# A two-layer graph network on one core: the routed experts' surroundings worked by groups of tiles, layer 1 fed from DRAM, edge terms as pairs of 64 rows in two places

## The chip, the cores and the metric

The kernel runs on one core of a Trainium2 chip. The core has five engines with a queue each, worked in order: PE (matrix products and transposes), DVE (vector work from SBUF and PSUM), ACT (copies, activations, and DMA issues), POOL (here mostly indirect DMAs: row gathers and scatters) and SP (DMA issues). [...] The metric is the device time of one execution in microseconds (us), the median of the runs. All data and arithmetic here is f32. The engines' instruction streams are written in program order by the kernel's Python and scheduled at build: an instruction waits for a semaphore of what it depends on, and whatever stands behind it on its engine waits too.

## The reference

3125 nodes with 256 features, 100,000 edges sorted by destination, 64 attributes an edge. Two layers, each a residual block of graph network plus mixer, then a residual feed-forward block:

```
xn = layernorm(x)
x  = x + L0_gnn(xn, edges) + L0_mix(xn)            # layer 0
x  = x + L0_ffn(layernorm(x))                      # 16 experts, top 2
xn = layernorm(x)
x  = x + L1_gnn(xn, edges, edge_attr) + L1_mix(xn) # layer 1
x  = x + L1_ffn(layernorm(x))                      # half of the tokens
```

The expert block, for each token y (normed x):

```
logits = y @ gate_w + gate_b ; the two largest, softmax over the two -> w
moe    = sum over the two experts of w * (relu(y @ w1[e] + b1[e]) @ w2[e] + b2[e])
out    = layernorm(y + moe) * gamma + beta
```

Layer 1's graph network, 8 heads of 32:

```
q = xn@Wq.T + bq ; k = xn@Wk.T + bk ; v = xn@Wv.T + bv ; e = edge_attr@We.T
alpha = sum(q[dst] * (k[src] + e)) / sqrt(32), softmax over the edges of one dst -> w
out   = sum over edges of w * (v[src] + e)  +  xn@Wskip.T + bskip
```

Layer 1's mixer is a second-order attention: moments of keys and of pairs of keys with the values are summed over all nodes (eight heads, worked as two halves of 128 columns), then each node's query reads them; a projection is added to x.

## The kernel before

**Tiling.** The nodes form 25 tiles of 125, in seven groups (`k.groups`) of up to four tiles. The residual x lies in SBUF for the whole kernel as `xcur` [125, 25, 256].

**Layer 0** (0 to some 3607 us) is not touched except that what follows it queues on SP and POOL behind its last loads, stores and row gathers, where the loads of the next stage are issued among them.

**The expert block**, `l0_ffn_routed` (line 1442), works in stages that each finish all tiles before the next begins:
1. Statistics and norm of all 25 tiles into `acc`, transposes to `xT` (`ln_to_T`, line 108).
2. Gate: per tile three small products and a copy (`gate_logits`, line 1425), PE and DVE in turn.
3. Top 2 of 16 for all tiles (`top2`, line 1393); a product with a triangular matrix and one with ones give each token its position in its expert's list; `sloti` holds its row in `xs`, a DRAM table of 16 × 512 rows.
4. 50 scatters (line 284): tile by tile and choice by choice, POOL sends the 125 rows of `acc` to `xs`.
5. 16 experts: loads of the two weight matrices, of `b2` and of the expert's 512 rows `xe` (line 1523 transposes them), two products with a relu between, result stored to `ys` in DRAM. The row loads wait for all scatters.
6. 50 gathers from `ys` (line 1552), each into one of three buffers of 125x256, followed by a DVE multiply-add into `acc`.
7. `norm_into` (line 1559): statistics of all tiles, then per tile norm (DVE, line 103), gamma (DVE, 1572), beta (POOL, 1573) and the add into `xcur` (POOL, 1574).

**Between the blocks** `layer1` (line 2496) norms again, stores the rows to DRAM (`xtab`) and keeps the transposed columns `xT` in SBUF. `l1_gnn_slots` (line 1889) first makes the k/v table: per tile a product, a DVE add of the bias (line 1923), and per group a store of up to 1000 KB to `kvtab`, from two buffers.

**The slot stage** (4244 to 6641 us, `by_slots`, line 876). The nodes are sorted by degree into 25 tiles of 128 with a fixed number of edge slots each (`SLOTS`, 64 down to 22); in all 864 slots, worked in 64 steps of up to 16 slots. Per step and block of up to 8 slots:
- POOL gathers a k/v row per node and slot (line 637) into one of four buffers `kv` [128, 8, 512]; the step's edge attributes come by one gather `ea`.
- For each pair of slots `add_edges` adds e = edge_attr @ We.T to both k and v: a PE transpose of 128x128 (two slots × 64 attributes, line 1945), an ACT copy to SBUF (1947), a PE product of 128x512 (1948) with `weT`, and a DVE add over 128x1024 (1953). `weT` is [128, 2, 256]: We in rows 0 to 63 for the first slot, in rows 64 to 127 for the second, zeros elsewhere. The product's tile `e` [128, 2, 256] is one bank by its size; the pool `e_pe` has two buffers of it, and the transpose is written to the same tile's first 128 columns.
- DVE multiplies by q (928), sums per head (932), and after softmax pieces (max, ACT exp, sum at 955) multiplies v (961) and folds it in half (966); PE sums the slots in `acc` with identity products (968).

A tile's rows for q and skip are gathered from `xtab` and transposed in the same pool's buffer (line 861 copies them).

**Beside** the slots runs the mixer, `l1_mix_pairs` (line 2201), a generator whose units are issued between the steps: it reads `xT` (SBUF) for k, v and q, keeps its moments in PSUM (`pairs`, `mom`), and adds its result to `xcur` (line 2414). Its products of 32-row blocks stand at line 2388; line 1968 is the graph network's skip product.

**Finish.** `finish` loads the graph network's result from DRAM (`gout`), seven `part` loads of 500 KB, and adds it to `xcur`; then the last feed-forward block (6681 to 6989 us).

[...]

Of the kernel before, what the change touches and what calls it, by code (L numbers as in the profile page):

```python
# [107 lines left out]
def ln_to_T(k, pool, pp, src, dstT, g=None, b=None, keep=None, rows=None):  # L108
# [4 lines left out]
    for g0, ng in k.groups:  # L113
# [7 lines left out]
        if rows is not None:  # L121
            nc.sync.dma_start(tok(rows)[:, g0 : g0 + ng], xh[:, :ng])
# [1270 lines left out]
def top2(k, one, lg):  # L1393


    nc, NT, NE = k.nc, k.NT, 16
    io = one.tile([P, NE], F32, name="io")
    nc.gpsimd.iota(
        io, pattern=[[1, NE]], base=-64, channel_multiplier=0, allow_small_or_imprecise_dtypes=True
    )  # L1400
    iob = io.unsqueeze(1).to_broadcast([P, NT, NE])
    oh = [one.tile([P, NT, NE], F32, name=f"oh{r}") for r in range(2)]
    mx = [one.tile([P, NT], F32, name=f"mx{r}") for r in range(2)]
    at = one.tile([P, NT], F32, name="at")
    for r in range(2):
        nc.vector.tensor_reduce(mx[r], lg, axis=AX.X, op=ALU.max)
        nc.vector.tensor_tensor(
            oh[r], lg, mx[r].unsqueeze(2).to_broadcast([P, NT, NE]), op=ALU.is_equal
        )
        nc.vector.tensor_tensor(oh[r], oh[r], iob, op=ALU.mult)  # L1410
        nc.vector.tensor_reduce(at, oh[r], axis=AX.X, op=ALU.min)
        nc.vector.tensor_tensor(
            oh[r], iob, at.unsqueeze(2).to_broadcast([P, NT, NE]), op=ALU.is_equal
        )
        if r == 0:
            nc.vector.scalar_tensor_tensor(lg, oh[0], -BIG, lg, op0=ALU.mult, op1=ALU.add)
# [5 lines left out]
    return oh, mx  # L1422
# [19 lines left out]
def l0_ffn_routed(k, dram, xcur, a, over):  # L1442
# [3 lines left out]
    NE = 16  # L1446
    ns = CAP // 128
    xs = dram.tile([NE * CAP, D], F32, name="xs")
    ys = dram.tile([NE * CAP, D], F32, name="ys")
    with ExitStack() as st:  # L1450
        big, one, wts, wp, hp, pp = pools(
            k, st, [("f_big", 1), ("f_one", 1), ("f_w", 3), ("f_wk", 3), ("f_hid", 2)], [("f_ps", 2)]
# [7 lines left out]
        xT = big.tile([128, 2, N], F32, name="xT")  # L1460
        ln_to_T(k, wp, pp, xcur, xT, keep=acc)
        lg = gate_logits(k, pp, one, xT, a)
        oh, mx = top2(k, one, lg)

# [6 lines left out]
        sel = one.tile([P, NT, NE], F32, name="sel")  # L1471
        nc.vector.tensor_tensor(sel, oh[0], oh[1], op=ALU.add)
        flat = sel.rearrange("p i e -> p (i e)")
        within = pp.tile([128, 512], F32, name="tp", tag="tp")
        nc.tensor.matmul(within[:P, : NT * NE], tri, flat, start=True, stop=True)
        total = pp.tile([128, 512], F32, name="o", tag="o")
        nc.tensor.matmul(total[:P, : NT * NE], ones, flat, start=True, stop=True)
# [5 lines left out]
        for i in range(NT):  # L1483
            nc.vector.tensor_tensor(
                base[:, i + 1], total[:P, i * NE : i * NE + NE], base[:, i], op=ALU.add
            )
        full = one.tile([P, NE], F32, name="full")
# [3 lines left out]
        pos = one.tile([P, NT, NE], F32, name="pos")  # L1491
        nc.vector.tensor_tensor(
            pos.rearrange("p i e -> p (i e)"), within[:P, : NT * NE],
            base[:, :NT].rearrange("p i e -> p (i e)"), op=ALU.add,
        )
        slot = one.tile([P, 2, NT], F32, name="slot")
        sloti = one.tile([P, 2, NT], I32, name="sloti")
        for r in range(2):
            nc.vector.tensor_tensor(oh[r], oh[r], pos, op=ALU.mult)
            nc.vector.tensor_reduce(slot[:, r], oh[r], axis=AX.X, op=ALU.add)  # L1500
        nc.vector.tensor_scalar_min(slot, slot, NE * CAP - 1.0)
        nc.vector.tensor_copy(sloti, slot)
        index = [sloti[:, r, i : i + 1] for i in range(NT) for r in range(2)]
        sent = scatter_rows(k, xs, index, [acc[:, i] for i in range(NT) for r in range(2)])
# [3 lines left out]
        stored = []  # L1508
        for e in range(NE):
# [26 lines left out]
            for i in range(ns):  # L1536
                ps = pp.tile([128, 512], F32, name="o", tag="o")
                for j in range(4):
# [5 lines left out]
            stored.append(  # L1544
                nc.scalar.dma_start(
                    ys[e * CAP : e * CAP + CAP, :].rearrange("(p i) d -> p i d", p=128), ye
                )
            )
        for i in range(NT):
            for r in range(2):  # L1550
                g = wp.tile([P, D], F32, name="g", tag="g")
                nc.gpsimd.indirect_dma_start(
                    out=g, out_offset=None, in_=ys,
                    in_offset=bass.IndirectOffsetOnAxis(ap=sloti[:, r, i : i + 1], axis=0),
                )
                nc.vector.scalar_tensor_tensor(
                    acc[:, i], g, mx[r][:, i : i + 1], acc[:, i], op0=ALU.mult, op1=ALU.add
                )
        norm_into(k, one, wp, acc, xcur, a)
# [20 lines left out]
def l0_ffn(k, xcur, a):  # L1580
    nc, N, NT = k.nc, k.N, k.NT
    NE = 16
    with ExitStack() as st:
# [11 lines left out]
        oh, mx = top2(k, one, lg)  # L1595
# [293 lines left out]
def l1_gnn_slots(k, dram, xT, xtab, xcur, order, edge_attr, a, beside):  # L1889

    nc, N = k.nc, k.N
    kvtab = dram.tile([N, 2 * D], F32, name="kvtab3")
    gout = dram.tile([len(SLOTS) * 128, D], F32, name="gout3")
    sent = []
    with ExitStack() as st:
        (one,) = pools(k, st, [("e_one", 1)])

# [4 lines left out]
        weT = one.tile([128, 2, D], F32, name="weT")  # L1902
        nc.gpsimd.memset(weT, 0.0)
        for b in range(2):
            nc.sync.dma_start(weT[b * 64 : b * 64 + 64, b], a["We"])
        with ExitStack() as s2:
            pw, wp, pp = pools(k, s2, [("e_pw", 1), ("e_st", 2)], [("e_pps", 4)])
            wkv = pw.tile([128, 2, 2 * D], F32, name="wkv")
            bkv = pw.tile([P, 2 * D], F32, name="bkv")
            for j, nm in enumerate("kv"):  # L1910
                nc.sync.dma_start(
                    wkv[:, :, j * D : j * D + D], a["W" + nm].rearrange("(c p) m -> p c m", p=128)
                )
                nc.sync.dma_start(bkv[:, j * D : j * D + D], a["b" + nm].partition_broadcast(P))
            for g0, ng in k.groups:
                t = wp.tile([P, 4, 2 * D], F32, name="st", tag="st")
                for j in range(ng):
                    i = g0 + j
                    ps = pp.tile([128, 512], F32, name="mm", tag="mm")
                    row_matmul(  # L1920
                        k, ps[:P], lambda c: xT[:, c, i * P : i * P + P], lambda c: wkv[:, c], None, 2
                    )
                    nc.vector.tensor_tensor(t[:, j], ps[:P], bkv, op=ALU.add)
                nc.sync.dma_start(tok(kvtab)[:, g0 : g0 + ng], t[:, :ng])

        with ExitStack() as s2:
            ep, kp, gp, wp, pe, po, pq = pools(
                k, s2,
                [("e_ea", 2), ("e_k", 2), ("e_g", 4), ("e_wk", 2)],
                [("e_pe", 2), ("e_po", 1), ("e_qa", 1)],  # L1930
            )

# [262 lines left out]
def l1_mix_pools(k, st):  # L2195
    return pools(
        k, st, [("q_one", 1), ("q_wk", 2), ("q_x", 1), ("q_sq", 3)], [("q_ps", 1), ("q_a", 1), ("q_b", 1)]
    )


def l1_mix_pairs(k, xT, xcur, a, pl):

# [415 lines left out]
```

## Time and profile before

| what | us |
|---|---|
| median of three runs (lowest, highest) | 6989.09 (6963.92, 7031.13) |
| profiled execution | 6991.24 |
| its span | 6989.4 |
| layer 0 | 0 to 3607 |
| norm, gate, top 2, positions | 3607 to 3691 |
| scatters, load of the first rows | 3691 to 3772 |
| 16 experts | 3772 to 4024 |
| gathers | 4024 to 4110 |
| norm, norm and transposes, k/v table | 4110 to 4244 |
| slot stage with the mixer | 4244 to 6641 |
| finish | 6641 to 6681 |
| last feed-forward block | 6681 to 6989 |

Over the span PE is busy 69%, DVE 63%, POOL 43%, ACT 22%; the mean granted PE clock is 0.80 of full speed. How to read the views that follow: in a row of windows each engine has its busy time and its number of instructions in that stretch; "PEclk" is the granted clock. A row of a tile or group gives line, engine, operation, output and inputs by the program's names, count; then busy time and mean ns of one, then the engine's idle time just before these instructions and who ended it. A wait reads: engine, what it wanted, who released it: sum in us, count, longest. A timeline row: start, duration, instruction; in brackets the idle time ahead of it and its releaser. An f32 product is recorded as two passes (x2, and x864 for 432 products).

### The profile page before, as it was taken

The numbers are of one execution on the slowest core, as the hardware profiler recorded it, in microseconds if no ns is written. First come the engines' busy times: TensorE is split into PE (matmuls) and PEld (weight loads), VectorE is DVE, ScalarE is ACT, GpSimd is POOL, SyncE is SP. The second block draws the span as 40 slices with busy tenths as digits, with TensorE's granted clock in tenths as the row PEclk, the third lists the DMA queues.
The fourth block names the chain that finished last, engine by engine and source line by source line (L and its number), as shares of the span: only waits on it lengthen the run. The fifth ranks groups of instructions, "written<-read, shape, count | busy, mean of one in ns | idle before, by whom it ended". The sixth has DMA issues, their size and how long they took to land. (4 is left out here: it accounts for less than half of the span.)

```text
span 6989.4 us, 48160 instructions
## 1 busy us (share of the span) xinstructions
PE 4802.1 (69%) x15661; PEld 2724.5 (39%) x15661; DVE 4388.0 (63%) x6132; ACT 1553.8 (22%) x3122; POOL 2991.1 (43%) x3084
## 2 busy tenths in 40 slices
PE   3445786577855687667834917777787787777738
PEld 2233554344533455444522602333333333333315
DVE  5367677666657777776731154656777765777771
ACT  2111223222412233323320101222112222212111
POOL 2456565555464565555433043333434433443310
PEclk9766898788877898788956957778778888888769
DMA  4356555555454565555433324333334433343310
GB/s 135 97 156 181 157 166 164 155 155 147 146 170 143 166 177 171 157 166 160 151 131 100 118 78 128 114 100 98 113 96 119 118 101 102 114 117 112 102 40 19
DMA packets 358262, 898.56 MB, mean 129 GB/s; under 512 B 93718, under 2 KB 150650, under 8 KB 357876
## 3 DMA queue, kind: packets, MB, share of 16 engines
q0 software_dynamic: 241376, 750.90, 37.1%
q1 hardware_dynamic: 109236, 123.30, 5.5%
q10 hardware_dynamic: 7390, 21.19, 0.8%
q8 instruction: 127, 2.08, 0.1%
q14 instruction: 133, 1.09, 0.1%
HBM read 816.51 MB, written 78.50 MB: 128 GB/s over the span
## 5 line engine op out<-in xcount | busy, mean ns | idle before, releaser
L637 POOL DMA_INDIRECT kv<-kvtab,slots x2592 | 2521.2, 973 | 2425.5 <-PE acc L968 827.4
L928 DVE TENSOR_TENSOR kv<-kv,qa 128x2048 f32<-128x2048 f32 (+1 forms) x351 | 741.3, 2114 | 327.4 <-DMA kv<-kvtab,slots 252.6
L1953 DVE TENSOR_TENSOR kv<-kv,e 128x1024 f32<-128x1024 f32 x432 | 519.4, 1214 | 361.4 <-PE e L1948 218.6
L932 DVE TENSOR_REDUCE al<-kv 128x32 f32<-128x2048 f32 (+3 forms) x351 | 738.2, 2112 | 1.5
L1948 PE MATMUL e<-weT,eaT 128*128 128x512 f32 x864 | 560.9, 746 | 184.7 <-ACT eaT L1947 110.4
L968 PE MATMUL cps<-kv,ident 128*128 128x256 f32 x1728 | 508.0, 449 | 155.3 <-DVE kv L966 91.4
L961 DVE TENSOR_TENSOR kv<-kv,qa 128x2048 f32<-128x2048 f32 (+1 forms) x234 | 489.5, 2113 | 0.0
L968 PEld LDWEIGHTS cps<-kv,ident 128*128 128x128 f32 x1728 | 378.5, 227 | 273.4 <-DVE kv L966 105.6
L142 PE MATMUL mm<-w,hid 128*125 128x256 f32 x1600 | 397.7, 399 | 57.9 <-issue 33.9
L1339 PE MATMUL mm<-hTm,w 128*128 128x500 f32 (+1 forms) x896 | 383.2, 586 | 25.0 <-issue 13.8
L966 DVE TENSOR_TENSOR kv<-kv 128x1024 f32<-128x1024 f32 (+1 forms) x351 | 389.2, 1134 | 0.0
L142 PEld LDWEIGHTS mm<-w,hid 128*125 128x125 f32 x1600 | 309.4, 197 | 141.7 <-issue 70.6
L1948 PEld LDWEIGHTS e<-weT,eaT 128*128 128x128 f32 x864 | 157.4, 218 | 410.4 <-issue 214.7
L968 PE MATMUL acc<-kv,ident 128*128 128x256 f32 x864 | 252.1, 454 | 70.1 <-DVE kv L966 69.6
L1339 PEld LDWEIGHTS mm<-hTm,w 128*128 128x128 f32 x896 | 173.7, 208 | 211.8 <-issue 183.8
L968 PEld LDWEIGHTS acc<-kv,ident 128*128 128x128 f32 x864 | 195.6, 232 | 154.0 <-DVE kv L966 103.6
L961 DVE TENSOR_TENSOR kv<-kv,al 128x2048 f32<-128x2048 f32 (+1 forms) x117 | 243.5, 2118 | 0.0
L142 PE MATMUL mm<-wqv,hTm 128*125 128x512 f32 x400 | 235.0, 698 | 12.2 <-DVE qs L1259 5.7
L1947 ACT COPY eaT<-e 128x128 f32<-128x128 f32 x432 | 107.2, 268 | 568.8 <-PE e L1945 269.1
L899 PE MATMUL qa<-wq,xpT 128*128 128x256 f32 x300 | 111.7, 506 | 133.5 <-ACT xpT L861 51.0
L972 ACT COPY res<-cps 128x256 f32<-128x256 f32 x128 | 47.6, 372 | 649.3 <-PE cps L968 433.3
L2388 PE MATMUL w<-x,sel 32*128 32x500 f32 (+3 forms) x448 | 161.9, 647 | 30.2 <-ACT sq L2393 14.8
(391 smaller groups left out, 7603.1 us busy)
## 6 DMA issues: line engine op xcount, KB each, us to landing
kv<-kvtab,slots POOLq DMA_INDIRECT x2592
w<-in_L_ffn_w_dram SPq DMA_DIRECT2D x32, 512.0 KB
qd<-qT ACTq DMA_DIRECT2D x24, 500.0 KB
kvtab<-st SPq DMA_DIRECT2D x12, 1000.0 KB
qT<-qd SPq DMA_DIRECT2D x24, 500.0 KB
w<-in_L_mix_W_dram SPq DMA_DIRECT2D x8, 1024.0 KB
xs<-zero SPq DMA_DIRECT2D x16, 512.0 KB
xe<-xs SPq DMA_DIRECT2D x16, 512.0 KB
```

What stands on the lines that cost most here:

```text
L142: nc.tensor.matmul(ps, lhs(c), w(c), start=(c == 0), stop=(bias is None and c == n_chunks - 1))
L637: return k.nc.gpsimd.indirect_dma_start(out=out, out_offset=None, in_=table, in_offset=bass.IndirectOffsetOnAxis(ap=index, axis=0),)
L899: nc.tensor.matmul(q, xpT[:, ci], wq[:, ci], start=(ci == 0), stop=False)
L928: nc.vector.tensor_tensor(kv[:, :m, :D], kv[:, :m, :D], q.unsqueeze(1).to_broadcast([128, m, D]), op=ALU.mult,)
L932: nc.vector.tensor_reduce(al[:, b0 : b0 + m], hv(kv[:, :m, :D]), axis=AX.X, op=ALU.add)
L961: nc.vector.tensor_tensor(v, v, w3[:, b0 : b0 + m].unsqueeze(3).to_broadcast([128, m, heads, d]), op=ALU.mult,)
L966: nc.vector.tensor_tensor(v, v, kv[:, m // 2 : m, D:], op=ALU.add)
L968: nc.tensor.matmul(acc[:, :D], k.ident, kv[:, j, D:], start=(b0 + j == 0), stop=(kv is bufs[-1][2] and j == m // 2 - 1),)
L1339: nc.tensor.matmul(ps[:, :w_], w1[:, c, j * 128 : j * 128 + 128], hT[:, c, :w_], start=(c == 0), stop=(c == 1),)
L1948: nc.tensor.matmul(e.rearrange("p b d -> p (b d)"), eaT, weT.rearrange("p b d -> p (b d)"), start=True, stop=True,)
L1953: nc.vector.tensor_tensor(t, t, e.unsqueeze(2).to_broadcast([128, 2, 2, D]), op=ALU.add)
L2388: nc.tensor.matmul(ps[:f, b, :w_], sel[rows, t * 128 : t * 128 + f], qT[rows, :w_], start=True, stop=True, tile_position=((h0 + b) * 32, 0),)
```

## The change

- **Expert block by groups.** Stages 1 to 4 above run group by group: statistics, norm, transposes, gate (the group's logits in one PSUM tile), top 2, positions (running sums `base`), and at once the group's eight scatters. Stages 6 and 7 too, with all that follows: per group eight gathers (eight buffers `f_back`), multiply-adds, statistics, norm with gamma and the add into `xcur` as two fused DVE operations, store of x, norm, store of rows, transposes, store of columns, k/v product and bias, store of k/v. Beta is added to `xcur` ahead of the experts, by seven POOL operations. The weights for k/v are loaded in front.
- **Layer 1 from DRAM.** `xcur` and `xT` are given up: the mixer loads each group's columns (`xTg`) and x (`xg4`) from DRAM and stores x back; the finish loads x beside `part` (three buffers for two).
- **Six gather buffers** `kv` in the slot stage, for four.
- **Edge terms.** `weT` holds We twice, without zeros, [128, 256]; the product of a pair is two products, rows 0 to 63 and rows 64 to 127, 256 columns each, into two banks. In place of two buffers there is one tile of two banks, `ee`, with two places of half of each bank, used in turn.

```diff
+        for g0, ng in k.groups:
+            g = slice(g0, g0 + ng)
+            mv, rs = group_stats(k, gp, xcur[:, g], ng)
+            for j in range(ng):
+                ln_tile(k, acc[:, g0 + j], xcur[:, g0 + j], mv, rs, j)
+            xT = group_T(k, gp, pp, acc[:, g], ng)
...
+            oh = top2(k, gp, io, lg, [m[:, g] for m in mx])
...
+            for i in range(g0, g0 + ng):
+                for r in range(2):
+                    ins = nc.gpsimd.indirect_dma_start(
+                        out=xs, in_=acc[:, i], in_offset=None,
+                        out_offset=bass.IndirectOffsetOnAxis(ap=sloti[:, r, i : i + 1], axis=0),
+                    )
...
+        for g0, ng in k.groups:
+            x = xcur[:, g0 : g0 + ng]
+            nc.gpsimd.tensor_tensor(x, x, bet.unsqueeze(1).to_broadcast([P, ng, D]), op=ALU.add)
...
+        for gi, (g0, ng) in enumerate(k.groups):
+            g = slice(g0, g0 + ng)
+            for i in range(g0, g0 + ng):
+                for r in range(2):
+                    got = bp.tile([P, D], F32, name="g", tag="g")
+                    gather(k, got, ys, sloti[:, r, i : i + 1])
                     nc.vector.scalar_tensor_tensor(
+                        acc[:, i], got, mx[r][:, i : i + 1], acc[:, i], op0=ALU.mult, op1=ALU.add
+                    )
+            mv, rs = group_stats(k, gp, acc[:, g], ng)
+            for j in range(ng):
+                i = g0 + j
+                nc.vector.scalar_tensor_tensor(
+                    acc[:, i], acc[:, i], mv[:, j, 0:1], gam, op0=ALU.subtract, op1=ALU.mult
+                )
+                nc.vector.scalar_tensor_tensor(
+                    xcur[:, i], acc[:, i], rs[:, j : j + 1], xcur[:, i], op0=ALU.mult, op1=ALU.add
+                )
+            nc.sync.dma_start(tok(tabs.x)[:, g], xcur[:, g])
...
+            nc.sync.dma_start(tok(tabs.rows)[:, g], acc[:, g])
+            xT = group_T(k, gp, pp, acc[:, g], ng)
+            nc.scalar.dma_start(tabs.cols[gi, :, :, : ng * P], xT[:, :, : ng * P])
...
+            nc.sync.dma_start(tok(tabs.kv)[:, g], t[:, :ng])
...
-                [("e_ea", 2), ("e_k", 2), ("e_g", 4), ("e_wk", 2)],
-                [("e_pe", 2), ("e_po", 1), ("e_qa", 1)],
-            )
+                [("e_ea", 2), ("e_k", 2), ("e_g", 6), ("e_wk", 2)],
+                [("e_pe", 1), ("e_po", 1), ("e_qa", 1)],
+            )
+            ee = pe.tile([128, 2, 2, D], F32, name="e")
+            turn = [0]
+            def place():
+                turn[0] ^= 1
+                return ee[:, :, turn[0]]
...
-                        e = pe.tile([128, 2, D], F32, name="e", tag="e")
+                        e = place()
                         nc.tensor.transpose(e[:, 0, :128], ea[:, c0 : c0 + 128], k.ident)
                         eaT = kp.tile([128, 128], F32, name="eaT", tag="eaT")
                         nc.scalar.copy(eaT, e[:, 0, :128])
-                        nc.tensor.matmul(
-                            e.rearrange("p b d -> p (b d)"), eaT, weT.rearrange("p b d -> p (b d)"),
-                            start=True, stop=True,
-                        )
+                        for b in range(2):
+                            half = slice(b * 64, b * 64 + 64)
+                            nc.tensor.matmul(e[:, b], eaT[half], weT[half], start=True, stop=True)
...
+            qT = unit_T(load_cols(gi, ng), c, ng, s, temp[:, c : c + 1])
+            x = ip.tile([P, 4, D], F32, name="xg4", tag="xg4")
+            nc.sync.dma_start(x[:, :ng], tok(tabs.x)[:, g0 : g0 + ng])
...
+                nc.vector.tensor_tensor(x[:, j], ps[:P, :D], x[:, j], op=ALU.add)
+            nc.sync.dma_start(tok(tabs.x)[:, g0 : g0 + ng], x[:, :ng])
...
+            k.nc.sync.dma_start(x[:, g0 : g0 + ng], tok(tabs.x)[:, g0 : g0 + ng])
+            after(k, k.nc.sync.dma_start(part[:, :ng], tok(gout[0 : k.N, :])[:, g0 : g0 + ng]), sent)
```

## The prediction

> **What bounds the kernel now.** I cut the span at the borders that the order of work draws and read the stages by windows first, because the page's averages mix them:
>
> ```profile
> core 0: us, PE busy (x) PEld busy (x) DVE busy (x) ACT busy (x) POOL busy (x), PEclk, DMA share, GB/s
> ...
> 3691.00:3772.00 81.00, 0.00 (x0) 0.00 (x0) 0.00 (x0) 0.00 (x0) 59.63 (x50) 0.50 0.33 90
> 3772.00:4024.00 252.00, 241.13 (x896) 160.80 (x896) 47.88 (x96) 45.25 (x65) 0.61 (x2) 0.99 0.39 128
> 4024.00:4116.00 92.00, 0.00 (x0) 0.00 (x0) 38.63 (x103) 0.32 (x1) 60.57 (x50) 0.50 0.32 79
> 4181.00:4244.00 63.00, 48.14 (x101) 19.69 (x101) 16.03 (x48) 3.94 (x11) 3.87 (x4) 0.86 0.37 133
> 4244.00:6641.00 2397.00, 1845.91 (x5396) 806.03 (x5396) 1658.34 (x1702) 507.64 (x1107) 944.65 (x976) 0.81 0.38 109
> ```
>
> To be seen: around the experts (3772 to 4024, PE full) lie two stretches in which PE does nothing and POOL's row transfers run alone, 81 and 92 us. The slot stage of layer 1 (4244 to 6641) is a third of the time, and no engine is full in it: PE 77%, DVE 69%.
>
> Then the two transfers, by tile:
>
> ```profile
> L284 POOL DMA_INDIRECT xs<-acc,sloti x50: 1184/1188/1414, 3691.1 to 3764.5; - x50
> L1552 POOL DMA_INDIRECT g<-ys,sloti x50: 1207/1211/1267, 4023.9 to 4109.5; - x50
> ```
>
> The scatters start 84 us after layer 0 ends (3607), since top-2 is done for all tiles at once; after the last gather come layer norms, transposes and the k/v table, to 4244.
>
> For the slot stage: its costly groups, DVE's and POOL's waits, and one pair in the timeline.
>
> ```profile
> L1948 PE MATMUL e<-weT,eaT 128*128 128x512 f32 x864 | 560.9, 746 | 184.7 <-ACT eaT L1947 110.4 <-issue 66.4 <-DMA kv<-kvtab,slots 6.4
> L1953 DVE TENSOR_TENSOR kv<-kv,e 128x1024 f32<-128x1024 f32 x432 | 519.4, 1214 | 361.4 <-PE e L1948 218.6 <-issue 52.9 <-remote 37.1
> ```
> ```profile
> DVE kv L1953 <- PE e L1948: 218.6, 86, 15.9
> DVE kvt L2273 <- PE pairs L2306: 63.8, 11, 18.4
> DVE den L955 <- ACT al L954: 45.0, 22, 7.7
> ...
> POOL kv L637 <- PE acc L968: 827.4, 53, 29.7
> ```
> ```profile
> 6386.88 0.27 PE L1945 MATMUL e<-ident,ea 128*128 128x128 f32 x1
> 6387.35 0.27 ACT L1947 COPY eaT<-e 128x128 f32<-128x128 f32 x1
> 6387.68 1.13 PE L1948 MATMUL e<-weT,eaT 128*128 128x512 f32 x2 [0.52 <-ACT eaT L1947]
> 6388.96 1.21 DVE L1953 TENSOR_TENSOR kv<-kv,e 128x1024 f32<-128x1024 f32 x1
> ```
>
> DVE idles 2397 − 1658 = 739 us here, half of it (361.4) before the edge adds, which wait for PE's edge product: DVE and PE take turns in a chain of transpose, copy, product, add, 432 times. POOL waits for buffers (827.4), but DVE hardly ever for a gather.
>
> **The change, part by part.** All against the profiled 6991.24 (span 6989.4 and 1.8 around it), 2.2 above the median 6989.09.
>
> *Ahead of the experts.* Per group of four tiles there are now stats, norm, transposes, gate, top-2, positions and at once eight scatters. The first group's chain: DVE about 10.4 us by the rows of these operations in 3607–3691, PE's gate 4 × 1.47 = 5.9, the rest transposes, two table loads on ACT (1.28 each) and hand-overs; I take 32 from layer 0's end at 3607, so the first scatter starts near 3639. DVE's 6.25 × 10.4 = 65 us then lie beside POOL's 50 scatters (1.19 and 0.30 until the next, 74.4). POOL also gets seven adds of beta (125x1024, 2.34 in such an add of layer 0), of which four stand ahead of the last scatters: 9.4. End 3639 + 74.4 + 9.4 = 3723; from the last scatter to PE's first transpose 6.5 as now (3765.7 to 3772.2): 3730 for 3772, **−42**. SP now has eight more loads ahead of layer 0's last stores and the experts' weights: up to 16 us late, I take 5. Together **−37**, bounds −60 (the first group takes little more than DVE's 10.4) and −10 (six more groups cost POOL 3 us each, and the loads their 16).
>
> *Behind the experts.* Now 220.6 us from 4023.9 to the first kv gather at 4244.5: gathers 86, norm 27, transposes 38, k/v table 52, 12 until its last store can be read, and hand-overs. After: DVE per tile two gathered adds 0.97, two statistics 1.17, two fused norm operations 0.98, a norm 0.41, the bias add 0.68: 4.2, × 25 = 105, and 7 + 5 + 12 to get in, drain and land: 129, −92. Against it the stores: on SP's queue x, rows and k/v, 12.8 MB where it has 9.6 now, and 3.2 of columns on ACT's; this is how the k/v store paces DVE now:
>
> ```profile
> 4208.02 2.48 DVE L1923 TENSOR_TENSOR st<-mm,bkv 125x512 f32<-125x512 f32 x4 [7.09 <-DMA kvtab<-st]
> 4216.03 2.48 DVE L1923 TENSOR_TENSOR st<-mm,bkv 125x512 f32<-125x512 f32 x4 [5.53 <-DMA kvtab<-st]
> ```
>
> 1000 KB in 8.0 us; SP's 12.8 MB make 102 us at that, and the gathers and columns share the DMA engines: 135, −85. I take **−85**, bounds −110 (gathers 86 and 24 behind them) and −50 (stores and gathers one after the other: 102 + 60.6, and the entry of 7).
>
> *Edge products.* Removed is half of each: the 128x512 product against a weight padded with zeros (two passes, 560.9 ÷ 432 = 1.30 a pair) becomes two 64-row products of 256 columns. That row blocks run side by side and 256 columns take half is seen here:
>
> ```profile
> 6399.24 1.03 PE L1968 MATMUL acc<-wsk,xpT 128*128 128x256 f32 x4
> 6407.83 2.04 PE L2388 MATMUL w<-x,sel 32*128 32x500 f32 x4 [0.69 <-ACT sq L2393]
> 6411.60 2.08 PE L1948 MATMUL e<-weT,eaT 128*128 128x512 f32 x2
> ```
>
> Each f32 product is two passes. Two products of 256 columns on 128 rows take 1.03, at a granted clock of 1.00 (window 6396 to 6400), one of 512 columns 1.13 at the same clock above. At 0.50 (6407 to 6414) two products of 500 columns on two 32-row blocks take 2.04, what one full one takes, 2.08: the blocks run beside each other. So a pair costs 0.65, **−280 us of PE's work**. This is not time yet: PE isn't full, and most of its work lies beside DVE's.
>
> Added is a wait. Before, two edge tiles of two banks each alternate: 416 of 432 transposes wait for the add of two pairs back. Now both places lie in one tile, each with half of both banks, and in the built program all 432 transposes wait for the add just before. What queues behind that transpose on PE: the mix's products, the folds into acc (which free POOL's buffers) and the next chunk's. So a loop from add to add replaces the alternation: transpose start to product end was 1.93 in the pair above, at full clock; with 0.60 for 1.13 it is 1.40, with a hand-over at each end about 1.6, at a clock of 0.50 about 2.2, with something queued ahead on PE or ACT 2.4 to 3. DVE can do other work in it: in the new DVE order only 65 of 431 adds follow another directly (111 before). Summing over all gaps what is missing with the row means of the DVE work that lies in each: idle 183 us for a loop of 1.6, 327 for 2.4, 474 for 3.0, 608 for 3.5. Against 361.4 now that is −178, −34, +113, +247. I take 2.4, the row's 1.93 shortened but queued on PE at two thirds load: −34.
>
> [...]
>
> Other DVE waits for PE and ACT (63.8 + 45.0 above and small ones, some 115) get shorter with 15% less work in PE's queue, and with adds that stand apart: I take **−40**, bounds 0 and −100.
>
> *Six gather buffers for four.* DVE's waits for kv gathers are some 12 us in the stage; nothing beyond the freedom that the new order already shows: 0, bounds −30 and 0.
>
> *Columns and x from DRAM.* The mix loads 28 column tiles and 14 x tiles of 500 KB and stores 14, 28 MB beside the stage's 2397 × 109 = 261 MB; the DMA share of 0.38 hides them. Two buffers, so a load has one unit to come; if 42 loads are late by some 0.4 us each, 5% of the 8.0 us that 1000 KB take: +15, bounds 0 and +60.
>
> Slot stage: −34 − 40 + 15 = **−60**, bounds −280 (all of PE's work returned) and +215.
>
> *Finish.* Now 40 us with seven loads of part; x has to be loaded too, 3.2 MB more on the same queue. In layer 0's tail a group with two loads takes 8.9 us: 7 × 8.9 = 62 less what the FFN's start hides, **+15**, bounds 0 and +30.
>
> Sum: 6991 − 37 − 85 − 60 + 15 = **6824**.
>
> **The rivals.**
> (a) PE is the real bound of the slot stage and returns all: −280 for −60, 6604. For: PE 77%, DVE's idle time names it. Against: the wait on the add puts DVE into PE's queue 432 times.
> (b) The other side: the two places act as one and the loop is 3.5 long because the transpose sits in PE's queue behind mix work that itself waits, so that DVE stands still in each gap. 608 − 361 = +247 in the stage, the rest −107: 7131. It decides from a loop of 3.0 (+113 cancels the rest). For: all 432 waits; the span from transpose start to product end has a median of 3.0 and a mean of 4.2 in this trace, with queueing. Against: DVE's new order puts other work into five gaps of six, and the PE queue gets shorter.
> (c) The change doesn't do what it says: the two 64-row products run one after the other, no PE work saved, four weight loads for two. Loop 2.8 to 2.9: idle 423 to 430, +65, others 0: 6991 − 107 + 65 = 6949. Against: the 32-row blocks above.
> (d) The surroundings give little: stores, columns and gathers collide, front −10, back −50, finish +30, with −30 in the slot stage: 6931.
>
> **How the numbers follow.** Forecast 0.52 (its own range 6720 to 6920), (a) 0.15, (b) 0.13, (c) 0.12, (d) 0.08. A measurement of this kernel tells 1% from no change: faster is under 6919, slower over 7059. Faster: nearly all of the forecast and (a), 0.65; same: (c), (d) and crumbs, 0.23; slower: (b), 0.12. The range runs from 6600, with (a), to 7010, with (c) and (d); (b) is left out.
>
> **What would show it.** First scatter near 3640, experts from about 3730, first kv gather about 135 us after the experts. Edge product two passes in about 0.6 us side by side. Idle before the edge add near 330; if over 470, (b). PE busy about 280 less in the slot stage; if not, (c). Waits of PE for columns above 60 us in all, or experts waiting for weights, would make it wrong too.

## The result, and the profile after

The changed kernel takes 7351.93 us (median of four runs, 7330.31 to 7373.28). The kernel before, run beside it, took 7005.14 (6963.92 to 7031.13). The ratio is 1.0501, 95% interval [1.0432, 1.0569]: **5% slower**, where 6824 was forecast. The profiled execution took 7330.31, its span 7328.4, 339 us more than the 6989.4 of before.

Where they came from, measured between the same events in both traces (layer 0's end is PE's last product before its long pause; the slot stage runs from the first edge add to the end of the last):

| stretch | before | after | change | forecast |
|---|---|---|---|---|
| layer 0's end to the experts' first product | 225.1 | 187.2 | −38 | −37 |
| experts | 246.4 | 246.5 | 0 | 0 |
| experts' end to the first edge add | 231.6 | 192.3 | −39 | −85 |
| slot stage | 2365.6 | 2807.2 | **+442** | −60 |
| finish and last feed-forward block | 373.6 | 370.3 | −3 | +15 |

The missing −22 is layer 0, which ended at 3525 for 3547. That isn't the change: five later profiles with the same surroundings, in series of the same length, had it at 3548 to 3576.

So the whole loss lies in the slot stage. Its windows after, the columns as before:

```profile
3525.00:3712.00 187.00, 55.78 (x229) 49.38 (x229) 66.70 (x285) 19.53 (x36) 91.66 (x67) 0.50 0.31 92
3712.00:3959.00 247.00, 241.34 (x896) 160.77 (x896) 48.02 (x100) 43.98 (x64) 0.00 (x0) 0.99 0.36 125
3959.00:4151.00 192.00, 80.97 (x173) 34.95 (x173) 90.83 (x298) 16.32 (x39) 73.56 (x62) 0.71 0.49 152
4151.00:6958.00 2807.00, 2142.87 (x6228) 930.11 (x6229) 1673.44 (x1683) 513.07 (x1100) 935.76 (x966) 0.67 0.35 102
```

The last row holds both surprises: PE's busy time in the stage rose (2143 us; in the same stretch of before, 4250 to 6616, it was 1829 at a clock of 0.81), though half of each edge product was taken away, and its granted clock fell to 0.67. DVE did the same work as before (1673 to 1636) in 441 us more.

The groups of the page for that stage, edge add, edge product and edge transpose:

```profile
L2043 DVE TENSOR_TENSOR kv<-kv,e 128x1024 f32<-128x1024 f32 x432 | 525.6, 1217 | 838.6 <-PE e L2041 349.0
...
L2041 PE MATMUL e<-weT,eaT 64*128 64x256 f32 x1728 | 442.6, 587 | 99.7 <-ACT eaT L2038 65.0
...
L2036 PE MATMUL e<-ident,ea 128*128 128x128 f32 x432 | 173.6, 402 | 320.3 <-DVE kv L2043 239.0
```

DVE's idle time ahead of the edge adds is 838.6 us for 361.4: that is the loss. And PE stands 239.0 us before transposes until an add is done, where before it hardly waited for one:

```profile
PE e L1945 <- DVE kv L1953: 31.1, 29, 3.4
```

The timeline after shows how the loop turns, near the stage's end (start, duration, instruction, idle time before it and its releaser):

```profile
6945.20 0.48 PE L2036 MATMUL e<-ident,ea 128*128 128x128 f32 x1 [1.40 <-DVE kv L2043]
6945.71 0.27 ACT L2038 COPY eaT<-e 128x128 f32<-128x128 f32 x1 [3.19 <-PE e L2036]
...
6946.03 1.22 PE L2041 MATMUL e<-weT,eaT 64*128 64x256 f32 x4 [0.35 <-ACT eaT L2038]
6947.36 1.22 DVE L2043 TENSOR_TENSOR kv<-kv,e 128x1024 f32<-128x1024 f32 x1
...
6948.64 0.48 PE L2036 MATMUL e<-ident,ea 128*128 128x128 f32 x1 [1.38 <-DVE kv L2043]
```

One engine works at a time: transpose, copy, products, add, then the next transpose 0.06 us after the add's end. The round takes 3.44 us, with nothing else in PE's queue, and PE runs at half clock (granted 0.50 from 6944 to 6950). A transpose behind a pause of PE takes 0.33 at full clock in this trace, 0.48 here; the four product passes 0.70 (at 5060, granted 1.00) and 1.22: 0.67 of the 3.44 us are the half clock's.

### The profile page after: what moved, and what is told of

The parts are those of the page before. It is cut to its first block, busy times and chain, and to the rows that moved or that the text cites. A ratio compares the mean times of both kernels' runs of the same rounds, so it can differ in the third digit from the quotient of the medians.

```text
span 7328.4 us, 50159 instructions
## 1 busy us (share of the span) xinstructions
PE 5115.8 (70%) x16549; PEld 2854.3 (39%) x16549; DVE 4414.9 (60%) x6270; ACT 1576.1 (22%) x3152; POOL 2977.2 (41%) x3040
## 5 line engine op out<-in xcount | busy, mean ns | idle before, releaser
L2043 DVE TENSOR_TENSOR kv<-kv,e 128x1024 f32<-128x1024 f32 x432 | 525.6, 1217 | 838.6 <-PE e L2041 349.0
L2041 PE MATMUL e<-weT,eaT 64*128 64x256 f32 x1728 | 442.6, 587 | 99.7 <-ACT eaT L2038 65.0
L2036 PE MATMUL e<-ident,ea 128*128 128x128 f32 x432 | 173.6, 402 | 320.3 <-DVE kv L2043 239.0
L966 PE MATMUL acc<-kv,ident 128*128 128x256 f32 x864 | 281.8, 494 | 91.3 <-DVE kv L964 87.2
L2041 PEld LDWEIGHTS e<-weT,eaT 64*128 64x128 f32 x1728 | 185.3, 255 | 358.4 <-issue 207.1
L2036 PEld LDWEIGHTS e<-ident,ea 128*128 128x128 f32 x432 | 71.5, 166 | 617.7 <-DVE kv L2043 356.4
L2475 PE MATMUL w<-x,sel 32*128 32x500 f32 (+3 forms) x448 | 263.4, 827 | 53.7 <-ACT sq L2480 38.8
L966 PEld LDWEIGHTS acc<-kv,ident 128*128 128x128 f32 x864 | 215.1, 256 | 174.6 <-DVE kv L964 110.3
L2382 PE MATMUL w<-sel,x 32*125 32x496 f32 x400 | 260.5, 952 | 20.8 <-issue 12.4
```

The costliest lines, as they stand in the source:

```text
L966: nc.tensor.matmul(acc[:, :D], k.ident, kv[:, j, D:], start=(b0 + j == 0), stop=(kv is bufs[-1][2] and j == m // 2 - 1),)
L2041: nc.tensor.matmul(e[:, b], eaT[half], weT[half], start=True, stop=True)
L2043: nc.vector.tensor_tensor(t, t, e.unsqueeze(2).to_broadcast([128, 2, 2, D]), op=ALU.add)
L2382: nc.tensor.matmul(ps[:P, b, :496], kT[rows, tk], sel[rows], start=True, stop=True, tile_position=((h0 + b) * 32, 0),)
L2475: nc.tensor.matmul(ps[:f, b, :w_], sel[rows, t * 128 : t * 128 + f], qT[rows, :w_], start=True, stop=True, tile_position=((h0 + b) * 32, 0),)
```

## The experiments

Three theories. **W**: the wait for the add just before, which the two places in the same two banks bring. **G**: the order that six gather buffers allow, or the columns and x from DRAM. **H**: the 64-row products themselves. The kernels ran in series, each beside the kernel before, and ratios are to the kernel before of the same series. It took 6327 and 6340 us in two of them ("transposes apart", "quads", "product twice" and "four gather buffers" with old edges; and the third run of the changed kernel with its neighbours: the short series) and 6981 to 7051 in the others, so times are compared within a series unless the text says otherwise.

### Undoing the edge terms, and doing them alone

**Old edge terms in the changed kernel.** Products of 128x512 against the padded weight, two tiles of one bank:

```diff
-                        e = place()
+                        e = pe.tile([128, 2, D], F32, name="e", tag="e")
...
-                        for b in range(2):
-                            half = slice(b * 64, b * 64 + 64)
-                            nc.tensor.matmul(e[:, b], eaT[half], weT[half], start=True, stop=True)
+                        nc.tensor.matmul(
+                            e.rearrange("p b d -> p (b d)"), eaT, weT.rearrange("p b d -> p (b d)"),
+                            start=True, stop=True,
+                        )
```

> The changed kernel, but the edge terms as before: zero-padded 128x512 products, two edge tiles of one bank each, used in turn. Its transposes wait for the add of two pairs back again (417 of 432). Theory W (the wait for the add just before, which the two places in the same two banks bring, makes PE, ACT and DVE take turns and lets PE's clock fall): the slot stage falls from 2829 us back to about 2390, the granted clock in it to about 0.80, and the gain of the surroundings (about 100 us to the first edge add) stays: 6860 to 6930. Theory G (the order that six gather buffers allow, or the columns and x from DRAM, make the slot stage slow): the stage stays near 2750, 7250 or more. Theory H (the 64-row products themselves are slow, with four weight loads for two): as W here.

Measured: 6940.80, ratio 0.9938 [0.9917, 0.9959]. Its slot stage:

```profile
4174.00:6548.00 2374.00, 1833.14 (x5342) 793.25 (x5342) 1639.22 (x1675) 503.95 (x1096) 936.38 (x964) 0.81 0.40 119
```

2374 us at a clock of 0.81, as before the change (2366, 0.81), though the six gather buffers and the loads of columns and x are in it. G falls. The time is 10 us above the forecast range, since the surroundings give some 77 us and not 100: the 100 held the 22 of layer 0.

**New edge terms alone, in the kernel before.** The reverse of that diff, plus the places:

> The kernel before with the new edge terms alone: 64-row pairs in two places of one tile; four gather buffers, columns and x in SBUF. All 432 transposes wait for the add just before. W: slot stage longer by 380 to 440 us, 7380 to 7440, clock near 0.67. G: within 1% of 6990 to 7005. H: as W.

Measured: 7442.40, ratio 1.0667 [1.0638, 1.0696]; slot stage 2819 us at 0.66. The edge terms bring the whole loss, and G is out from this side too.

**One edge tile in the kernel before**, and nothing else:

```diff
-                [("e_pe", 2), ("e_po", 1), ("e_qa", 1)],
+                [("e_pe", 1), ("e_po", 1), ("e_qa", 1)],
```

> The kernel before with one edge tile instead of two, nothing else: zero-padded 128x512 products, one bank. All 432 transposes wait for the add just before. W: as slow as the 64-row pairs or slower, since the product in the loop is longer (0.4 us at full clock, 0.8 at half): 7400 to 7600. H: near the time before, at most 7100, since the products are the old ones. G: as H.

Measured: 7347.15, ratio 1.0530 [1.0507, 1.0552]; slot stage 2720 us at 0.75. This kernel has the old products; all that is new is that each transpose waits for the add just before. That alone costs 366 us: W holds, and H cannot be the main cause. But the step "as slow or slower, since the product is longer" was wrong. The 64-row pairs, whose product takes 0.70 for 1.12 at full clock, were 95 us slower in the same series. In their run 243 of 432 transposes ran at half clock, here 148, in the kernel before 89. The lower clock may be the reason, or the pairs' four weight loads for two; no run tells these apart, and so some 95 of the 461 us that the new edge terms cost alone have no shown cause.

**Four gather buffers for six in the changed kernel.**

```diff
-                [("e_ea", 2), ("e_k", 2), ("e_g", 6), ("e_wk", 2)],
+                [("e_ea", 2), ("e_k", 2), ("e_g", 4), ("e_wk", 2)],
```

> The changed kernel with four gather buffers for six. W: within 1% of 7352, the buffers are not what the stage waits for; DVE's waits for gathers at most some 100 us more. G: the order of the adds goes back to that of before and the time falls by 200 us or more, if the six buffers are the cause.

Measured: 7409.59, ratio 1.0601 [1.0572, 1.0629]; slot stage 2869 us. The changed kernel itself has 1.0501 [1.0432, 1.0569], and in a later series 1.0557 [1.0520, 1.0594]: the two buffers are worth at most 1%, and the second interval overlaps with this one. Without the loop, in the changed kernel with the old edge terms and this last edit, they are worth nothing that shows:

> The changed kernel with the old edge terms and four gather buffers: what is left of the change are the experts' surroundings and layer 1 from DRAM. If six buffers matter only while the loop holds up the stage (as the run with four in the changed kernel showed, 60 us): within 0.5% of the one with six, 6900 to 6970. If they matter by themselves: 6990 to 7010.

Measured: 6267.66, ratio 0.9905 [0.9880, 0.9929], for 0.9938 and (below) 0.9915 with six. Its series was one of the two short ones, so the forecast times don't apply; the ratio does.

### What in the loop costs

**Transposes in a bank of their own.** The kernel before, its two banks used otherwise: one for all transposes, one for all products. Only the product waits for the add just before.

```diff
-                        nc.tensor.transpose(e[:, 0, :128], ea[:, c0 : c0 + 128], k.ident)
+                        eT = pe.tile([128, 2, D], F32, name="eT", tag="eT")
+                        nc.tensor.transpose(eT[:, 0, :128], ea[:, c0 : c0 + 128], k.ident)
```

> The kernel before with its two edge banks used otherwise: one only for the transposes, one only for the products. The product waits for the add just before, the transpose and the copy no longer do: of the loop of the one-buffer kernel (transpose, copy, product, add; slot stage 2720 us) transpose and copy with their hand-overs go, some 0.9 us of a pair. W (every link of the loop costs): between before and the one buffer, slot stage 2450 to 2600, 7060 to 7220. If any wait for the add just before is as bad as any other: 7300 or more.

Measured in a short series: 6436.44, ratio 1.0173 [1.0153, 1.0193].

**Both places filled at once ("quads").** The changed kernel, but two transposes, one copy and four 64-row products fill both places, and then two adds of 128x1024 empty them: the same work in 234 rounds for 432.

```diff
+                        for u in range(n):
+                            nc.tensor.transpose(ee[:, 0, u, :128], ea[...], k.ident)
+                        nc.scalar.copy(eaT[:, :n], ee[:, 0, :n, :128])
...
+                        for h in range(2):
+                            t = kv[:, j : j + 2 * n, h * D : h * D + D].rearrange("p (u b) d -> p u b d", b=2)
+                            nc.vector.tensor_tensor(t, t, e, op=ALU.add)
```

> The changed kernel, but both places are filled before any add: two transposes, one copy, four 64-row products, then two adds of 128x1024 (one for the keys, one for the values of four slots). The same work in about half as many rounds of the loop (234 for 432, by the pairs left over in blocks of six slots). W: the hand-overs and the waiting per round halve, slot stage 2550 to 2700 for 2807, 7090 to 7240, clock not above 0.67. If the 64-row products themselves are the cost: unchanged, 7350.

Measured in the same short series: 6472.81, ratio 1.0235 [1.0215, 1.0254], at a clock of 0.75 in the stage, where no more than 0.67 was expected. Neither had its counterpart in that series; the four kernels side by side:

> The changed kernel again, beside the next one, for the comparison on one chip in one call: 1.05 to 1.056 of before, slot stage 2800 to 2890 us.

> Both places filled before two adds: 234 rounds of the loop for 432. If the price lies in the rounds (hand-overs and waiting per round): at least a third of the 440 us that the slot stage lost comes back, 150 us or more below the changed kernel. If it lies in PE's lower clock alone: the clock stays below 0.70 and less than 60 us come back.

> One edge tile, beside the next one: 1.048 to 1.053 of before.

> One bank for the transposes, one for the products: only the product waits for the add just before. If every link of the loop costs alike, transpose and copy with their hand-overs (0.9 of 3.0 us in the median round of one edge tile) are a third of the loss: 1.03 to 1.04 of before. If it matters more that PE can transpose ahead while an add runs: 1.02 or less.

Measured, the kernel before at 6340.44:

| kernel | time | ratio [95%] | slot stage | clock in it |
|---|---|---|---|---|
| changed | 6784.93 | 1.0710 [1.0685, 1.0734] | 2589 | 0.69 |
| quads | 6478.43 | 1.0220 [1.0197, 1.0243] | 2309 | 0.74 |
| one edge tile | 6810.21 | 1.0756 [1.0719, 1.0792] | 2539 | 0.77 |
| transposes apart | 6450.17 | 1.0190 [1.0160, 1.0220] | 2177 | 0.86 |

Half the rounds bring 280 us of the stage's time back, with the same products and as much to add: the price lies in the rounds, the clock's part in it included (0.74 for 0.69). With transpose and copy out of the loop 360 of the 470 us that the one edge tile costs are gone, far more than their share of 0.9 in 3.0 us. That is the second case of the expectation, in which it matters more that PE can transpose ahead while an add runs; a third of the links was the wrong measure. The changed kernel and the one edge tile lost more here (7%) than the 1.05 expected from the longer series; why isn't shown.

### The clock

PE pauses in each round. Does that lower the clock, and does the clock cost time? In the kernel with one edge tile a bank is left over. Into it each product is made a second time, read by nobody:

```diff
+            junk = pe.tile([128, 2, D], F32, name="junk")
...
+                        nc.tensor.matmul(
+                            junk.rearrange("p b d -> p (b d)"), eaT, weT.rearrange("p b d -> p (b d)"),
+                            start=True, stop=True,
+                        )
```

> The kernel before with one edge tile, and each product made a second time into the bank that is left over, read by nobody: 432 more products, about 1.1 us each at full clock, 475 us more of PE's work. Theory W with the clock as its amplifier (PE's pauses in the loop lower the clock, and the lower clock makes the loop longer): clock in the slot stage above 0.85 for 0.75, and the stage not longer than the 2720 of the one buffer, perhaps 2550 to 2720: 7180 to 7350. W without the clock (the loop's waits alone): the work comes on top where it doesn't fit under the adds, 7400 to 7600.

Measured in the first short series: 6799.48, ratio 1.0752 [1.0731, 1.0773]. Then side by side, with the kernel before and the changed one again, all four as already described:

> The kernel before, unchanged, for its profile on the same chip as the next three: the chip of the second four runs took 6327 us for it where the first took 6981. On the faster chip its slot stage is expected near 2090 us, as in the run with old edge terms and four gather buffers (2079), with no idle time in which an engine waits for nothing that the profile shows; on the first kind of chip 2366.

> The changed kernel, on one chip with the next two. Theory W: slower than before on any chip. On the first kind 1.05 of before; on the faster one the run with both places filled at once was 1.024, and this one is slower than that: 1.03 to 1.06.

> One edge tile instead of two, on one chip with the run that makes each product twice. If PE's pauses lower the clock and the clock makes the loop longer: not faster than that run by more than 1%, though it has 432 products less, and its slot stage at a clock lower by 0.1 or more. If the loop's waits alone count: faster than it by 100 us or more.

> One edge tile, each product made twice, the second read by nobody. With the clock as amplifier: within 1% of the one without the second products, clock in the slot stage 0.90 to 0.93 (0.92 in the run before). Without: slower than it by 100 to 250 us.

Measured, the kernel before at 7051.19 (7048.74 as a run of its own, slot stage 2413): the changed kernel 7445.29, ratio 1.0557 [1.0520, 1.0594]; one edge tile 7401.04, 1.0478 [1.0446, 1.0509]; product twice 7431.12, 1.0541 [1.0511, 1.0571]. Windows of the slot stage, the first of the kernel with one edge tile:

```profile
4278.00:7031.00 2753.00, 2104.92 (x5361) 872.95 (x5362) 1670.56 (x1682) 512.27 (x1100) 933.29 (x969) 0.75 0.32 95
```

and of the one that makes each product twice:

```profile
4285.00:7066.00 2781.00, 2269.26 (x6226) 964.45 (x6225) 1674.30 (x1682) 507.58 (x1100) 940.23 (x969) 0.88 0.32 94
```

432 more products, an estimated 475 us of work at full clock (1.1 us each; the rows below have 1.02 and 1.13), lengthen the stage by 28 us; PE's busy time grows by 164 only, since the clock rises from 0.75 to 0.88 (0.90 to 0.93 was expected) and the same work on PE gets shorter (a transpose 0.325 us in the mean for 0.369, a pass of the edge product 0.729 for 0.831). In the two short series the stages were 2539 at 0.77 and 2537 at 0.92. So in this kernel the clock rises when PE's pauses are filled. Two rounds with nothing else in PE's queue show that it costs time: one edge tile at half clock ("one edge tile in the kernel before"), then the product made twice at full clock.

```profile
6938.81 0.48 PE L1945 MATMUL e<-ident,ea 128*128 128x128 f32 x1 [1.31 <-DVE kv L1953]
...
6939.69 2.07 PE L1948 MATMUL e<-weT,eaT 128*128 128x512 f32 x2 [0.41 <-ACT eaT L1947]
6941.80 1.22 DVE L1953 TENSOR_TENSOR kv<-kv,e 128x1024 f32<-128x1024 f32 x1 [3.05 <-PE e L1948]
...
6943.08 0.48 PE L1945 MATMUL e<-ident,ea 128*128 128x128 f32 x1 [1.31 <-DVE kv L1953]
```
```profile
7043.77 0.33 PE L1947 MATMUL e<-ident,ea 128*128 128x128 f32 x1 [0.45 <-DVE kv L1959]
...
7044.51 1.13 PE L1950 MATMUL e<-weT,eaT 128*128 128x512 f32 x2 [0.41 <-ACT eaT L1949]
...
7045.47 1.02 PE L1954 MATMUL junk<-weT,eaT 128*128 128x512 f32 x2
...
7045.67 1.22 DVE L1959 TENSOR_TENSOR kv<-kv,e 128x1024 f32<-128x1024 f32 x1 [1.96 <-PE e L1950]
...
7046.95 0.33 PE L1947 MATMUL e<-ident,ea 128*128 128x128 f32 x1 [0.46 <-DVE kv L1959]
```

The round takes 4.27 us at half clock, and 3.18 at full clock with the second product in it: that one ends at 7046.49, before the add does (7046.89), as in 356 of the 432 rounds. So the second product is hidden in two ways, by the clock that it raises and by the add that it runs under. What the slow clock costs over the whole stage can't be read from a sum in which both stand. It is an amplifier and not the cause: at 0.88 and 0.92, above the 0.81 of before, the loop still costs 5 to 7%.

How long a pause has to be isn't to be read from these traces. In the changed kernel's rounds shown above PE pauses for 1.4 us at a time, and the clock stays at half for round after round (transposes of 0.48 from 6931 to 6949, granted clock 0.50). By the clock records of the same trace the clock fell to half 113 times in the slot stage; PE's longest pause in the 10 us before a fall was 1.4 us in the median, 0.3 at one end and 4.3 at the other. From 4950 to 4968 it was granted 1.00 throughout, over a pause of 2.9 us (4955.2 to 4958.1). The pause's length alone didn't decide it here.

### The stores behind the experts

The stage behind the experts gave 39 us for the forecast 85. SP's queue in it (changed kernel):

```profile
4023.17 9.43 SPq L1662 DMA_DIRECT2D kvtab<-st  x1
4032.68 6.87 SPq L1654 DMA_DIRECT2D xtab<-acc  x1
4039.66 15.21 SPq L1650 DMA_DIRECT2D x<-xcur  x1
```

Each of these issues holds the queue for 7 to 15 us; DVE waits for the stores of k/v (23.9 us) and, at the end, for x to leave SBUF (24.1):

```profile
DVE i L2253 <- DMA x<-xcur: 24.1, 1, 24.1
DVE st L1661 <- DMA kvtab<-st: 23.9, 3, 11.0
```

One store of three was moved to ACT's queue, in the kernel with the old edge terms, which was run beside it:

```diff
-            nc.sync.dma_start(tok(tabs.x)[:, g], xcur[:, g])
+            nc.scalar.dma_start(tok(tabs.x)[:, g], xcur[:, g])
```

> The changed kernel with the old edge terms and six gather buffers, and the store of x behind the experts on ACT's queue: SP's has 1500 KB a group for 2000, ACT's 1000 for 500. If SP's queue sets the stage: from the experts' first product to the first edge add some 20 to 35 us less than in the next run, and the time by that much. If DVE's chain or the DMA engines as a whole set it: within 10 us.

> The changed kernel with the old edge terms, for the comparison: 0.99 of before, and about 439 us from the experts' first product to the first edge add where the calls take some 7000 us for the kernel before, less where they take 6330.

Measured, the kernel before at 7007.67: 6946.90, ratio 0.9913 [0.9887, 0.9939], and 6962.65, 0.9915 [0.9887, 0.9943]. From the experts' first product to the first edge add 432.6 and 443.1 us. The 10 us lie at the border of what was expected if SP's queue doesn't set the stage, and the nine profiles of kernels with these surroundings and all three stores on SP themselves range from 438 to 447. SP's issues got no shorter either (8 to 14 us each behind the first, for fewer bytes), so the queue is not the bound alone; what is left are the DMA engines as a whole or DVE's chain, and no run tells these apart.

## Why the prediction was wrong

Point by point, in its own order:

- **Ahead of the experts: right.** −37 forecast, −38 measured. The first scatter came 95.5 us after layer 0's end for 144.0 (−48; −52 by the step), and the scatters took 83.9 us for 73.4 because POOL waits for groups and adds beta (+10; +9.4 by the step).
- **Behind the experts: the mechanism right, a term too small.** DVE's 105 us were 91; between the forecast's own borders, the first gather to the first kv gather, 135 were forecast and 179 came. The term that was too small is the stores: DVE waits 48 us for them (23.9 and 24.1). Only SP's 12.8 MB were set against the rate of 1000 KB in 8.0 us, the columns on ACT's queue and the gathers were put down as 33 us on top. All stores together, 16 MB, make 128 us at that rate, before any gather. The last experiment agrees that another queue buys little; what limits the stores is open.
- **PE's work: the overlap right, its size and what it buys wrong.** The row halves do run beside each other: four passes take 0.70 at full clock, where four one after the other took 1.03 in the prediction's row of L1968. So rival (c) is out. But 0.70 is 0.62 of the full product's 1.13 and not half; by these rows 432 pairs save an estimated 186 us at full clock, not 280. And the prediction held the clock still: the products' busy time fell by 118 us (442.6 for 560.9), while PE's whole busy time in the stage rose by 314, with the rest of its work at a clock of 0.67 for 0.81.
- **The loop: this is the step that failed.** "I take 2.4, the row's 1.93 shortened but queued on PE", and with it −34 us. Measured from the end of an add to the end of the next product the mean is 4.20 us (median 3.54). In the kernel before the same distance is 1.39, because the next product is mostly under way when an add ends. The step took transpose to product's end (mean 2.87, median 2.05, so not far off) and left out the first part: after an add the next transpose starts 1.33 us later in the mean, since PE has turned to other work meanwhile. On the other side the add waits 1.13 us behind other work of DVE. In one buffer's loop these delays add up; the round is 2.87 + 1.13 + 1.22 + 1.33 = 6.55, and one add comes every 6.51 us (5.49 before). The table of idle time over loop lengths was sound: worked out in the same way from the trace after, a loop of 4.20 makes 823 us of idle time, and 838.6 were measured.
- **Other DVE waits:** DVE's idle time apart from that before the edge adds fell from 369 to 295 us. −40 was forecast, −74 came; no run shows whether for the reasons given.
- **Columns and x from DRAM: not contradicted.** With old edge terms the slot stage took 2374, 2383 and 2397 us; the kernel before took 2366 and 2413. So +15 can't be told from nothing.
- **Finish:** +15 forecast, −3 measured. The seven loads of x were issued at 6676 to 6698, 260 us before the stage's end, and had long landed; only the part loads are seen.
- **Rival (b)** named the mechanism, the sign and the point from which it decides (a loop of 3.0), and had a transpose-to-product mean of 4.2 from the trace as evidence. It was set aside because other work fills most gaps between the adds. That work doesn't shorten the loop: it stands in the loop, as the 1.13 and the 1.33 us above. Its price of 7131 was low by 221, of which 195 lie in the slot stage (+247 for +442): its loop was 3.5 us for 4.20.

## What to carry to other kernels

In this built program two places in the same PSUM banks are one buffer for PE and DVE; a program without these waits wasn't run, so whether the hardware needs them is not shown here. Before exchanging two tiles for two halves of a larger one, read in the built program whose end each write waits for, and if it is the reader just before, price the whole round. For such a round across three engines don't take the shortest pass through it: add what each engine's queue puts between two links, and look whether PE's clock falls when PE pauses in each round (here from 0.81 in the stage to 0.75 with one edge tile, to 0.67 in the changed kernel). Halving an operation of an engine that waits bought nothing here: with the shorter product the loop cost 95 us more than with the long one, at a lower clock (0.66 for 0.75). The part of the change that paid was the one that put work beside lone transfers: with the old edge terms it is 0.6 to 1% faster than the kernel before.

## What was not expected of the hardware

Making every product twice cost almost nothing (28 us for some 475 us of work, and 2 us less between the two short series): the clock rose with it (0.75 to 0.88, 0.77 to 0.92), and most of the second products ran under the add (356 of 432 ended before it did).

The same program took 10% less in two of the series. The profiles of one edge tile show where: of 606 us, 395 lie ahead of layer 0's end (3577 for 3182) and 214 in the slot stage. There DVE has 227 us, ACT 460 and PE 207 of idle time in the long series for which no releaser shows ("issue" and "remote"); in the short one 7, 0 and 0. One expectation above puts it down to the chip; but one of the short series and the one of 7051 us ran on the same chip. What makes these stalls is not known from these runs.
